# One rare-case block in place of two, and three reorderings, in a graph, attention and expert layer on one core

## The chip, the cores and the metric

The kernel runs on one core of a Trainium2 chip. The metric is the device time of one execution in microseconds (us). Before the change the median of three runs is 1005.16 us (1004.86 to 1005.45).

The engines of the core are named as in the profile: PE (TensorE, matrix products), with PEld for its weight loads; DVE (VectorE); ACT (ScalarE); POOL (GpSimd); SP (SyncE, which here only issues DMAs). A `q` after a name is that engine's instruction queue.

## The reference

The layer takes 625 nodes with 1024 features and 20000 edges (`src`, `dst`, sorted by `dst`).

```python
xn = layernorm(x)
x = x + gnn(xn, src, dst) + mix(xn)
x = x + ffn(layernorm(x))

# gnn: two layers, mean over the incoming edges
agg = segment_sum(h[src], dst); mean = agg / max(deg, 1)
h = relu(xn @ W_self0 + mean(xn) @ W_neigh0 + b0)
out = h @ W_self1 + mean(h) @ W_neigh1 + b1

# mix: linear attention, 16 heads of 64
q = softmax(x @ Wq, over a head's 64) / 8;  k = softmax(x @ Wk, over the nodes);  v = x @ Wv
out = (q @ (k.T @ v)) @ Wo + bo

# ffn: 8 experts, the best 2 of each node, and a shared expert
routed = sum over the node's 2 experts of p * (silu(xf @ w1[e]) @ w2[e])
shared = sigmoid(xf @ shared_gate_w) * ((silu(gate) * up) @ shared_down)
```

## The kernel before, in words

**Numbers in two parts.** Every operand of the large products is split into a high part, which ACT casts, and a low part, which DVE (in the experts' inputs POOL) makes by a subtraction. `split`, line 99, does both, so line 99 stands for a great many instructions that differ by their tile: `whi` and `wlo` are the two parts of a weight tile, `xnh` and `xnl` those of the normalised features, `xfh` and `xfl` those of the expert stage's input, `xs` those of an expert's rows, `he` those of an expert's hidden values. Each product is three matmuls: high by high, low weight by high, high weight by low.

**Weights.** All weights come from HBM in tiles of 512 KB through one list, `Stream`. SP issues the loads (line 121) into three buffers `wraw`; in the expert stage three more, `wmore`, are used in turn. `whi` and `wlo` have three buffers each. A load waits until a buffer's last reader, as a rule a `wlo` subtraction, is done.

**Order.** A scheduler fixes the order of instructions on every engine when the kernel is built, from priorities and the dependencies. Some instructions are held in the order of the program (`keep_in_program_order`, `keep` in the first stage), and `issue_after` puts one behind another. At run time each engine takes its queue in order. PSUM has eight banks which go round (`bank`), and the pool `tmp` has five buffers.

**Stages in order of time.**
1. Start (lines 433 to 462). The five node tiles are normalised (`first_stats`, `first_scale`, `first_norm`) and turned: `first_turn` calls `to_t` (line 283), which for each half g of the features does four PE transposes (line 288) into a bank and one `split` into `xnh`, `xnl`. Between them `keys_steps` runs pieces of the key product: `keys_step(s)` (lines 391 to 414) is twelve matmuls over four of the eight feature blocks, lines 405 to 407. The first steps need only node tiles 0 and 1 (256 columns) and run before the others are there. `keys_weights` takes a weight tile; the fourth goes into a tile named `fourth`. `turn_edges` (line 357, bank `psed`) turns the edge list. The last row of `x` is a DMA of its own (line 314).
2. One-hot counts of the edges (lines 485 to 539) among the rest of the key product and layer 0's self product. The counts are packed into `ath`, from which `dinv` and `degs` (inverse degrees) come. They are right unless two rare conditions hold, and `rare` is then not zero.
3. Queries, values, and the heads' 128 by 128 context blocks `cbd` (lines 742 to 749, bank `psc`).
4. **First If, line 752:** if `rare` is not zero, `recount` counts the edges anew with wider fields, and `inverse` makes the inverse degrees again. `values_load` (line 751) puts `rare` into a register of every engine. With the inputs here `rare` is zero and every engine jumps over the block.
5. `neighbours` (line 758): the product with `W_neigh0`, matmuls of `ts_half`, lines 209 to 211, bank `psg`.
6. Attention output (line 787), then the output projection (lines 801 to 813, bank `pso`). After its half 1, tile u=1, `low_step` is called: **second If, line 772**, which adds what the low parts of the counts contribute to layer 0, if `rare` is not zero. Besides, POOL loads rows of `x` into `xr` (line 809), adds the biases (line 810), and DVE adds the product (line 811).
7. Aggregation of layer 0 (line 828, bank `psag`), layer 1, with a third If at line 857.
8. The second layernorm; the shared expert's gate and up products (`ws_tile`, lines 226 to 228, banks `psga` and `psup`). Their columns come in two groups, node tiles 0 to 2 and tiles 3 and 4; tile 4 is turned last, right before the second group. Then `logits` (router and shared gate, `rwp` and `rwz`, bank `psr`, to `lgt`) for two column ranges `PARTS`, 0 to 313 and 314 to 625, then the routing.
9. The experts in the order `RANKS` = 0, 1, 2, 6, 3, 4, 5, 7 of their load, with room for 224 rows (ranks 0 to 2), 160 (3 to 5) or 128 (6, 7). `expert_wide` (lines 1193 on) takes ranks 0 to 5. Its first part forms the hidden values from w1 in four quarters (lines 1211 and 1215, bank `pse`); for each quarter `set` gathers the sum, then Silu, then `he` is split (lines 1220 to 1229). Its second part multiplies by w2 in two halves of four tiles, u = 0 to 3 (lines 1269 to 1271, bank `psy`; line 1246 for the rows beyond 128). A fourth If (line 1304) lies in the first expert.
10. The shared expert's down product and the final sums.

**The turns of the next expert's rows.** `Turn` (line 1016) holds the rows of the next expert. For a wide expert `Turn.step` does a DVE transpose of a block into `raw` (line 1046), and with the next step an ACT cast and a POOL subtraction into `xs`, line 99. A 224-row turn has two blocks of 512 columns and two of 384, a 160-row turn two of 512 and two of 128. The program calls `step` before each w2 tile of the running expert but the first. The scheduler is free as to where among DVE's other work the transposes go, as long as they keep their order.

## Time and profile before

| | us |
|---|---|
| median of three runs | 1005.16 |
| the profiled execution, its own time | 1006.07 |
| its span, first to last instruction | 1004.5 |
| PE busy | 994.2 |
| DVE busy | 601.4 |
| ACT busy | 394.4 |
| POOL busy | 144.5 |

The profiled execution took 0.91 us more than the median, and 1.57 us of it lie outside the span. The busy time of an engine is the time in which it has an instruction at work. A list of waits sums, for an engine and a line, the idle time before its instructions and names what ended it; `DVEq` or `PEq` with a line is the queue of that engine at a branch there. In a timeline row stand the start, the duration, the engine, the line, the operation with its tiles, a count if several equal ones follow each other, and in brackets the idle time before it. Matmuls overlap in the hardware, so the distance of two starts is what one costs, and it is shorter than the duration shown.

### The profile page before, as it was taken

To read this page: it belongs to the slowest core of one execution; us is meant where nothing else is said; L and a number is where in the kernel's file an instruction comes from. 1 tells how busy PE (TensorE), PEld (TensorE's weight loads), DVE (VectorE), ACT (ScalarE), POOL (GpSimd) and SP (SyncE) were. 2 spreads that over 40 slices of the span, in tenths; PEclk is the share of its full clock that TensorE was granted. 3 is DMA by queue.
4 is the path that set the end of the run, shared out by engine and by line. 5 is a ranking of instruction groups with operands and counts; after the bars stand their busy time and mean duration, and the time that the engine had idled before them with its cause. 6 is when DMAs were issued, how large, how long until landed. Compare 5 with 4: busy or idle time off the path is not lost. (4 is left out here: it accounts for less than half of the span.)

```text
span 1004.5 us, 14780 instructions
## 1 busy us (share of the span) xinstructions
PE 994.2 (99%) x5547; PEld 860.1 (86%) x5547; DVE 601.4 (60%) x1215; ACT 394.4 (39%) x577; POOL 144.5 (14%) x206
## 2 busy tenths in 40 slices
PE   9999999999999999999999999999999999999998
PEld 6999998888887779888878999997978787887886
DVE  7998745682333346423338355367678788877682
ACT  5533242231123212222116242265557576766610
POOL 1000011120100432200001002223032203110040
PEclk9999999999999999999999999999999999999999
DMA  8222227762321343322220125766977997887961
GB/s 238 60 65 64 85 100 257 251 235 86 95 84 64 105 157 124 124 83 84 66 82 2 46 81 173 241 205 207 266 244 217 292 357 237 280 297 253 339 249 64
DMA packets 111596, 164.69 MB, mean 164 GB/s; under 512 B 5948, under 2 KB 63686, under 8 KB 111512
## 3 DMA queue, kind: packets, MB, share of 16 engines
q1 hardware_dynamic: 97864, 118.38, 36.7%
q0 software_dynamic: 13456, 45.08, 13.6%
q8 instruction: 46, 0.75, 0.3%
q14 instruction: 38, 0.31, 0.1%
q10 hardware_dynamic: 192, 0.16, 0.0%
HBM read 133.19 MB, written 30.42 MB: 163 GB/s over the span
## 5 line engine op out<-in xcount | busy, mean ns | idle before, releaser
L99 DVE TENSOR_TENSOR wlo<-wraw,whi 128x1024 fp32r<-128x1024 f32 x148 | 186.0, 1257 | 247.0 <-ACT whi L99 237.8
L99 ACT CAST whi<-wraw 128x1024 fp32r<-128x1024 f32 x148 | 155.5, 1051 | 288.1 <-PE psg L211 76.2
L1215 PE MATMUL pse<-xs,whi 128*128 128x448 f32 (+1 forms) x384 | 109.2, 357 | 0.0
L99 DVE TENSOR_TENSOR wlo<-wmore,whi 128x1024 fp32r<-128x1024 f32 x67 | 82.1, 1226 | 25.8 <-ACT whi L99 23.3
L1211 PE MATMUL pse<-xs,wlo 128*128 128x224 f32 (+1 forms) x384 | 89.5, 254 | 0.6 <-DVE wlo L99 0.6
L99 ACT CAST whi<-wmore 128x1024 fp32r<-128x1024 f32 x67 | 70.4, 1051 | 42.5 <-PE psz L211 18.3
L405 PE MATMUL psk<-xnh,whi 128*128 128x384 f32 (+3 forms) x240 | 74.5, 312 | 0.3 <-ACT xnh L99 0.3
L406 PE MATMUL psk<-xnl,whi 128*128 128x384 f32 (+3 forms) x240 | 73.5, 306 | 0.6 <-DVE xnl L99 0.6
L407 PE MATMUL psk<-xnh,wlo 128*128 128x384 f32 (+3 forms) x240 | 73.5, 306 | 0.0
L1211 PEld LDWEIGHTS pse<-xs,wlo 128*128 128x128 f32 x384 | 72.0, 190 | 1.6 <-DVE wlo L99 0.8
L1215 PEld LDWEIGHTS pse<-xs,whi 128*128 128x128 f32 x384 | 69.1, 189 | 2.4
L1269 PE MATMUL psy<-whi,he 128*128 128x512 f32 (+1 forms) x176 | 69.5, 395 | 0.7 <-PEq L1304 0.7
L1270 PE MATMUL psy<-wlo,he 128*128 128x512 f32 (+1 forms) x176 | 69.4, 394 | 0.7 <-DVE wlo L99 0.7
L1271 PE MATMUL psy<-whi,he 128*128 128x512 f32 (+1 forms) x176 | 69.0, 392 | 0.0
L488 DVE TENSOR_SCALAR hot<-iota,srow,unit 125x128 f16<-125x128 f16 x160 | 49.6, 310 | 0.0
L406 PEld LDWEIGHTS psk<-xnl,whi 128*128 128x128 f32 x240 | 45.5, 190 | 0.8 <-DVE xnl L99 0.8
L405 PEld LDWEIGHTS psk<-xnh,whi 128*128 128x128 f32 x240 | 45.4, 190 | 0.6 <-ACT xnh L99 0.6
L407 PEld LDWEIGHTS psk<-xnh,wlo 128*128 128x128 f32 x240 | 45.4, 189 | 0.0
L99 POOL TENSOR_TENSOR xs<-raw,xs 128x512 fp32r<-128x512 f32 (+2 forms) x24 | 28.3, 1182 | 110.0 <-ACT xs L99 109.6
L487 DVE TENSOR_SCALAR hot<-iota,edt 125x128 f16<-125x128 f16 x160 | 39.8, 250 | 4.1 <-PE pa L505 4.1
L1269 PEld LDWEIGHTS psy<-whi,he 128*128 128x128 f32 (+1 forms) x176 | 31.9, 181 | 10.8 <-issue 1.1
L1270 PEld LDWEIGHTS psy<-wlo,he 128*128 128x128 f32 (+1 forms) x176 | 31.8, 181 | 10.0 <-DVE wlo L99 1.7
(361 smaller groups left out, 2367.2 us busy)
## 6 DMA issues: line engine op xcount, KB each, us to landing
wraw<-in_L_ffn_w_dram SPq DMA_DIRECT2D x65, 512.0 KB, 5.1
wmore<-in_L_ffn_w_dram SPq DMA_DIRECT2D x63, 512.0 KB, 5.2
xsd<-zt POOLq DMA_DIRECT2D x9, 1024.0 KB
wraw<-in_L_gnn_W_self_dram SPq DMA_DIRECT2D x16, 512.0 KB, 3.6
wraw<-in_L_gnn_W_neigh_dram SPq DMA_DIRECT2D x16, 512.0 KB, 3.8
wraw<-_ffn_shared_gate_up_dram SPq DMA_DIRECT2D x16, 512.0 KB, 3.9
wraw<-in_L_mix_Wk_dram SPq DMA_DIRECT2D x8, 512.0 KB, 6.7
wraw<-in_L_mix_Wq_dram SPq DMA_DIRECT2D x8, 512.0 KB, 3.6
```

Source lines behind the costliest of these rows:

```text
L99: return (order(nc.scalar.copy(hi, srcap)), order((eng or nc.vector).tensor_sub(lo, srcap, hi.bitcast(F32))))
L405: nc.tensor.matmul(ps[:, :n], wh[:, kt, :], xnh[:, kt, c], start=kt == 0, stop=False)
L406: nc.tensor.matmul(ps[:, :n], wh[:, kt, :], xnl[:, kt, c], start=False, stop=False)
L407: nc.tensor.matmul(ps[:, :n], wl[:, kt, :], xnh[:, kt, c], start=False, stop=kt == KT - 1)
L487: nc.vector.tensor_scalar(h[:ET, :WIN], iota[:ET, :WIN], edst[e], None, op0=ALU.is_equal)
L488: return nc.vector.tensor_scalar(h[:ET, WIN:], iota[:ET, :WIN], srow[e], unit[e].bitcast(F32), op0=ALU.is_equal, op1=ALU.mult)
L1211: nc.tensor.matmul(ps[a][:, :n], wl[:, k, c], xs[:, kt, 0, :], start=False, stop=False)
L1215: nc.tensor.matmul(ps[a][:, :2 * n], wh[:, k, c], xs[:, kt], start=kt == 0, stop=kt == KT - 1)
L1269: nc.tensor.matmul(acc, h(kt, 0), wh[:, k, :], start=kt == 0, stop=False)
L1270: nc.tensor.matmul(acc, h(kt, 0), wl[:, k, :], start=False, stop=False)
L1271: nc.tensor.matmul(acc, h(kt, 1), wh[:, k, :], start=False, stop=kt == KT - 1)
```

## The change

It has four parts.

1. The If at line 752 is taken out, and its content goes into the If in the output projection, which is now `rare_step`. The load of `rare` into the registers stands after `neighbours`. The block's code becomes shorter: the loop over the eight feature blocks is a loop at run time (`For_i`) with a copy `go` of the operand, and `recount` takes the degrees from a `reduce_sum` of the counts instead of matmuls over reloaded low parts. With these inputs the block is not entered, so what is in it is jumped over before and after.
2. `logits` takes the ranges as an argument. The first range is called right after tile 4 is turned, ahead of the second column group of gate and up; the second range stands where both stood.
3. In the start the first two tiles are turned half by half (tile 0 and 1 of g=0, then of g=1) instead of tile by tile; the first two key steps do the four matmuls of high by high, then the four with the low weights, then the four with the low features, instead of the three in turn for each block; and the second weight tile is taken before the statistics of node tile 2.
4. A DVE transpose of `Turn.step` is put behind the low part of the last weight tile taken (`st.low`) and behind the low part of the running expert's last `he` (`behind`).

In the instruction orders that the build gives, PE, DVE, ACT, POOL and SP differ around these places. Three of the moves are not in the diff's text. On SP the fifth load of `Wk` stands ahead of the one-row load of `x`, where it stood behind it. On PE four more matmuls on `fourth` stand ahead of tile 3's transposes. On ACT the square root for tiles 3 and 4 stands behind the first cast of tile 2's turn. In the experts the transposes, which stood among the additions into `set` and the `he` low parts, stand in one row behind them and behind `wlo` of w2's tile u=2, directly ahead of `wlo` of u=3; ACT's casts and POOL's subtractions of `xs` follow them.

```diff
-            split(r, hi, lo, eng, **order)
+            self.low = split(r, hi, lo, eng, **order)[1].ins
...
-    def to_t(nat, t, hi, lo, order=None, both={}):
-        for g in range(2):
+    def to_t(nat, t, hi, lo, order=None, both={}, parts=(0, 1)):
+        for g in parts:
...
-        for kt in range(4 * h, 4 * h + 4):
-            nc.tensor.matmul(ps[:, :n], wh[:, kt, :], xnh[:, kt, c], start=kt == 0, stop=False)
-            nc.tensor.matmul(ps[:, :n], wh[:, kt, :], xnl[:, kt, c], start=False, stop=False)
-            nc.tensor.matmul(ps[:, :n], wl[:, kt, :], xnh[:, kt, c], start=False, stop=kt == KT - 1)
+        kts = range(4 * h, 4 * h + 4)
+        terms = ((wh, xnh), (wh, xnl), (wl, xnh))
+        if s < 2:
+
+            order = [(kt, *terms[j]) for j in (0, 2, 1) for kt in kts]
+        else:
+            order = [(kt, *term) for kt in kts for term in terms]
+        for j, (kt, w, xt) in enumerate(order):
+            nc.tensor.matmul(ps[:, :n], w[:, kt, :], xt[:, kt, c], start=h == 0 and j == 0,
+                             stop=h == 1 and j == len(order) - 1)
...
-        first_turn(0)
-        first_turn(1)
+        for g in range(2):
+            for t in range(2):
+                first_turn(t, (g,))
+        keys_weights(1)
         first_stats(2)
-        keys_weights(1)
...
+            nc.vector.reduce_sum(degs[:, 0, ds(r, 1)], acc, axis=AX.X)
...
-        for t in range(NT):
-            pt = bank("psdt")
-            for s in range(NT):
-                al = tmp.tile([128, T], F32R, name="al", tag="tmp")
-                nc.gpsimd.dma_start(al[rows(s), rows(t)], atd[cols(s), cols(t)])
-                nc.tensor.matmul(pt[rows(t), :2], ath[rows(s), s, cols(t)], ones[rows(s), :2], start=s == 0, stop=False)
-                nc.tensor.matmul(pt[rows(t), :2], al[rows(s), rows(t)], ones[rows(s), :2], start=False, stop=s == NT - 1)
-            nc.vector.tensor_copy(degs[rows(t), 0, t:t + 1], pt[rows(t), 0:1])
...
-    rare_v = nc.values_load(rare[0:1, 0:1], min_val=0, max_val=2)
-    with tc.If(rare_v > 0, preferred_fallthrough_block=False):
-        recount()
-        inverse(0, NT - 1)
-        inverse(NT - 1, 1)
...
     neighbours(xnh, xnl, g0h, g0l)
-    def low_step(half, u, accs):
+    rare_v = nc.values_load(rare[0:1, 0:1], min_val=0, max_val=2)
+
+    def rare_step(half, u, accs):
...
         with tc.If(rare_v > 0, preferred_fallthrough_block=False):
+            recount()
+            inverse(0, NT - 1)
+            inverse(NT - 1, 1)
             for s in range(NT):
                 al = low_part(s)
-                for o in range(KT):
+                with tc.For_i(0, KT, 1) as o:
+                    go = tmp.tile([128, 128], F32R, name="go", tag="tmp")
+                    nc.scalar.copy(go[rows(s), :], g0h[rows(s), s, ds(o * 128, 128)].bitcast(F32))
...
-    def logits():
-        for c0, n in PARTS:
+    def logits(parts):
+        for c0, n in parts:
...
     to_t(by_k(xfn[rows(4), 4, :]), 4, xfh, xfl)
+
+    logits(PARTS[:1])
     ga.append(bank("psga"))
     up.append(bank("psup"))
     ws_tile(xfh, xfl, ga[1:], SPARTS[1:], w=wg)
     ws_tile(xfh, xfl, up[1:], SPARTS[1:], w=wu)
-    logits()
+    logits(PARTS[1:])
...
+            self.behind = st.low
...
-                tc.keep_in_program_order(nc.vector.transpose(
-                    raw.rearrange("p k (t r) -> p t k r", r=32), rows[:, :, k]))
+
+                with tc.issue_after(st.low), tc.issue_after(self.behind):
+                    tc.keep_in_program_order(nc.vector.transpose(
+                        raw.rearrange("p k (t r) -> p t k r", r=32), rows[:, :, k]))
...
-                    nc.vector.tensor_sub(h2[:, :, b0:b0 + m], s[:, :, a0:a0 + m], h2[:, :, a0:a0 + m].bitcast(F32))
+                    low_he = nc.vector.tensor_sub(h2[:, :, b0:b0 + m], s[:, :, a0:a0 + m], h2[:, :, a0:a0 + m].bitcast(F32))
             else:
-                split(s, h2[:, :, :n], h2[:, :, n:])
+                low_he = split(s, h2[:, :, :n], h2[:, :, n:])[1]
         nxt = nxt()
+        nxt.behind = low_he.ins
```

More of the change, by code (lines that the diff above doesn't have):

```diff
@@ L342, in first_norm, with first_turn @@
             keep(nc.scalar.activation(xts[p, t, :], xts[p, t, :], AF.Identity, bias=z, scale=y))
-    def first_turn(t):
-        return to_t(xts[rows(t), t, :].rearrange("p (k c) -> p k c", c=128), t, xnh, xnl, keep, dict(order=keep))
+    def first_turn(t, parts=(0, 1)):
+        return to_t(xts[rows(t), t, :].rearrange("p (k c) -> p k c", c=128), t, xnh, xnl, keep, dict(order=keep), parts)
     edges = edgep.tile([EP, 2, 2 * ET], F32, name="edges")
@@ L778, in low_step @@
                         c = slice(c0, min(c0 + n, N))
-                        nc.tensor.matmul(ps[:, :n], g0h[rows(s), s, o * 128:(o + 1) * 128], al[rows(s), c0:c0 + n],
-                                         start=True, stop=True)
+                        nc.tensor.matmul(ps[:, :n], go[rows(s), :], al[rows(s), c0:c0 + n], start=True, stop=True)
                         lt = tmp.tile([128, NP], F32, name="lt", tag="tmp")
                         nc.vector.tensor_mul(lt[:, c], ps[:, :min(n, N - c0)], dinv[:, c])
-                        nc.vector.tensor_add(hself[:, o, c], hself[:, o, c], lt[:, c])
+                        nc.vector.tensor_add(hself[:, ds(o, 1), c], hself[:, ds(o, 1), c], lt[:, None, c])
             hold(accs)
@@ L803, in gps_layer @@
         accs = [bank("pso") for _ in range(NT)]
-        ts_half(aoh, aol, accs, step=lambda u: low_step(half, u, accs))
+        ts_half(aoh, aol, accs, step=lambda u: rare_step(half, u, accs))
         for t in range(NT):
```

## The prediction

> **What bounds the kernel now.** The page's first two parts come first. They say whether one engine fills the span and at what clock.

> ```profile
> span 1004.5 us, 14780 instructions
> PE 994.2 (99%) x5547; PEld 860.1 (86%) x5547; DVE 601.4 (60%) x1215; ACT 394.4 (39%) x577; POOL 144.5 (14%) x206
> PEclk9999999999999999999999999999999999999999
> ```

> TensorE (PE) is busy for 99% of the span, and its granted clock stands in the highest digit throughout. No other engine passes 60%. So a change that leaves the executed matmuls as they are can win only what lies between matmuls. That the change leaves them can be read in the code: the block that it shortens isn't entered with these inputs (the trace has no instruction of `recount`), and the other three parts reorder. The next view is therefore the list of PE's waits: line, what it waited for, total us, times, longest.

> ```profile
> PE pswarm L252 <- DVE cold L249: 1.5, 1, 1.5
> PE psg L209 <- DVEq L752: 0.8, 1, 0.8
> PE psy L1270 <- DVE wlo L99: 0.7, 2, 0.4
> PE psy L1269 <- PEq L1304: 0.7, 1, 0.7
> ...
> PE psk L406 <- DVE xnl L99: 0.6, 1, 0.6
> ...
> PE pso L209 <- PEq L772: 0.5, 1, 0.5
> PE psk L405 <- ACT xnh L99: 0.3, 1, 0.3
> PE psga L226 <- ACT xfh L99: 0.2, 1, 0.2
> PE psga L227 <- DVE xfl L99: 0.2, 1, 0.2
> ```

> With 0.6 at line 1211 and 0.5 at line 857, not shown, that is the whole stock: 6.6 us. The change aims at the 0.8 (line 752), the two of the start (0.6 and 0.3), the two 0.2 of line 226/227 and the 0.7 of line 1270, 2.8 us as listed. A matmul's listed wait is shorter than what it costs in starts, as the timeline shows (start, duration, operation, idle before it), so I count by starts.

> ```profile
> 266.00 1.17 PE L746 MATMUL psc<-vnat,knat 128*128 128x128 f32 x9
> 267.99 0.47 PE L209 MATMUL psg<-whi,xnh 128*128 128x512 f32 x1 [0.82 <-DVEq L752]
> ...
> 372.43 0.50 PE L209 MATMUL pso<-whi,aoh 128*128 128x512 f32 x1 [0.54 <-PEq L772]
> ```

> **Part 1, one If in place of two.** Nine `psc` matmuls start 0.11 us apart from 266.00, so the next start was due at 267.00 and came at 267.99: 0.99 us lost at line 752. That goes. The If at line 772 remains: matmul 371.51 is followed by 372.43 where 0.23 is the rule, 0.70 lost, and the merged If stands there. The matmul that follows reads weights split long before, so nothing else is late there. Bounds: −0.70, what the shorter If costs, and −1.00; I take −0.99. The register loads of `rare` now come just before the merged block on every engine; ScalarE (ACT) and VectorE (DVE) have nothing due for over 5 us after their branches (next work at 371.9 and 373.0, branches before 367.6), and PE reached its compare at 367.7, 4 us before it mattered. GpSimd (POOL) stood 46.5 us at line 752 ahead of the first `xr` loads; that goes, and nobody waited for them. Its waits at line 772 (7.4 for DVE, 2.1 for PE) stay ahead of the second half's `xr`. Price of this queueing: 0, bounds 0 and +2.1, if PE's turn came to wait so.

> [...] The trace's two jumps, 0.99 and 0.70, both show a stall.

> **Part 2, half of the logits earlier.** After tile 4's transposes PE waits twice, 555.82 and 556.48.

> ```profile
> 555.82 0.38 PE L226 MATMUL psga<-xfh,whi 128*128 128x242 f32 x1 [0.19 <-ACT xfh L99]
> ...
> 556.48 0.38 PE L227 MATMUL psga<-xfl,whi 128*128 128x242 f32 x1 [0.17 <-DVE xfl L99]
> ```

> The excess over the rule of 0.11 is 0.35 and 0.33, together 0.68. The first half of the logits (columns 0 to 313, tiles 0 to 2, turned long before) is 16 matmuls of 0.145 us, 2.3 us of work that reads nothing of tile 4, and the stall needs about 1. `rwp` and `rwz` are ready at 550.7. So −0.68; bounds 0 (if a bank isn't free) and −0.68. The cover is the banks' earlier readers, which ended at 552.1 and 555.4; the second half's copy to `lgt` is no later.

> **Part 3, the start.**

> ```profile
> 13.52 0.38 PE L405 MATMUL psk<-xnh,whi 128*128 128x256 f32 x1 [0.34 <-ACT xnh L99]
> 14.47 0.38 PE L406 MATMUL psk<-xnl,whi 128*128 128x256 f32 x1 [0.56 <-DVE xnl L99]
> ...
> 17.31 0.45 PE L357 MATMUL psed<-ident,edges 80*125 80x80 f32 x3
> ...
> 24.49 0.81 DVE L340 TENSOR_SCALAR xts<-xts,lnt 128x1024 f32<-128x1024 f32 x1
> 25.88 1.52 PE L288 MATMUL pst<-ident,xts 128*128 128x128 f32 x13
> ```

> With half g=0 of both tiles first, ACT's first two casts of 0.51 from 11.91 end at 12.94, and the first matmul starts near 13.04 (before 13.52). The four `xnh` and four `wlo` products cover DVE's subtracts, which end at 15.02; 24 matmuls of 0.12 end at 15.92 where `psed` now starts at 17.31: PE is 1.39 ahead. But DVE is without a gap from 12.5 to 29.5. With the same instructions in another order `first_norm(3)` (line 340) still ends near 25.30, and tile 3's transposes behind it start at 25.3 to 25.6 against 25.88: about −0.38. The order after the change has four more `fourth` matmuls ahead of them (16, before 12), of which three fit, −0.36: −0.74 if DVE loses nothing. Two rows say that it may. ACT's square root for tiles 3 and 4 (22.46 before) now stands behind a cast of tile 2's turn, which PE reaches near 22.2: some +0.2. And SyncE's queue has the fifth `wk` load ahead of the last row of `x` (one row, issued at 12.81, landed at 17.9). That load waits for a `wraw` buffer, free when `wlo` of the second tile ends, now near 16.2, so the row is issued at 16.7; the 512 KB ahead of it took 3.4 to 4.9 us to land when issued at 17.57, so the row lands at 20 to 21.1. Its reader, the statistics of tile 4, stands at 20.95: late by 0 to 0.2. I take −0.5; bounds 0 and −1.39.

> **Part 4, turns behind low parts.** In a wide expert's w2 part, DVE does the next expert's transposes (line 1046), the set adds, `he` low parts and `wlo`; POOL subtracts `xs` low parts. PE stalls where `wlo` of the fourth tile (u3) is late: two places, 840.37 (0.53 by starts) and 875.80 (0.50), both with a 160-row host.

> ```profile
> 837.25 0.44 DVE L1046 STREAM_TRANSPOSE raw<-xb 128x128 f32<-128x128 f32 x1
> 837.62 1.55 DVE L1227 TENSOR_TENSOR he<-set,he 128x256 fp32r<-128x256 f32 x2
> ...
> 840.37 0.50 PE L1270 MATMUL psy<-wlo,he 128*128 128x512 f32 x1 [0.36 <-DVE wlo L99]
> ```

> Before, the transposes stand at 833.06, 834.32 and 837.25. Now they stand behind `wlo` of u2 and the last `he`, in one row ahead of `wlo` of u3. Worked forward from `whi` of u2 at 833.3 with these durations: `wlo` u2 to 835.6, `he` to 836.2, transposes 1.14 + 1.17 + 0.38 to 838.9. POOL's first `xs` subtract (1.31) then runs from 838.1 to 839.4. The trace shows what a POOL subtract does to a DVE operation beside it: the `he` pair took 1.55 with POOL's 2.14 at 836.95 beside it, and `wlo` at 735.66 took 1.53, where 1.2 is usual, with POOL's 1.36 running from 734.76. So `wlo` of u3 begins when POOL ends, and ends at 840.5, against need at 839.84: stall 0.7 in place of 0.53, +0.2 at each place. Without the clash it ends at 840.15, −0.15 each. Bounds for the two: −1.03 (all goes) and +1.8 (POOL's second subtract goes first too). I take +0.4. At the three 224-row hosts (`wlo` of u3 ended 692.01, 735.24 and 777.64, needed at 692.58, 735.81 and 778.98) the same row of transposes ends near 734.1 just as POOL's first subtract does: 0 if DVE gets in, stall 0.7 each at two places (third: slack 1.3) if POOL's second subtract does. I take 0; bounds −0.3 and +1.8.

> [...]

> **Sum.** −0.99 − 0.68 − 0.5 + 0.4 = −1.8. Unchanged are the waits of lines 857 and 1304, both ends of narrow experts and the warm-up. The profiled execution took 1006.07 (span 1004.5), 0.9 over the median of 1005.16; I subtract from the median: 1003.4.

> **The rivals.**
> 1. Everything aimed at goes: −0.99 − 0.68 − 1.39 − 1.03 = −4.1, 1001.1. For it: the parts each name a real wait. Against: DVE without a gap to 29.5, and transposes bunched ahead of the very `wlo` that was late.
> [...]
> 3. The start's gain is given back in full to DVE's chain, by the late row of `x` and the square root: −1.8 + 0.5 = −1.3, 1003.9.
> 4. Ends on the other side: the merged If holds up the output projection. POOL stands longer before the second half's `xr`, DVE's five additions of line 811 behind them keep PSUM banks from `psag`, and PE waits. Slower than before from 1.8 us lost there, at 6 us 1009. For it: DVE already waits 1.10 at 384.18 for a sum of POOL's. Against: PE shows no wait in this stretch after 372.43, and POOL is there first by the 46.5 us won.

> **How the numbers follow.** Chances: forecast 0.45 (own range 1002.4 to 1004.4), rival 1 0.17, rival 2 0.18, rival 3 0.12, rival 4 0.08. A measurement tells from no change what is over 0.2%, here 2.0 us: below 1003.15 is faster, above 1007.17 slower. Faster: nearly half of the forecast's and all of rival 1's, 0.38. Slower: most of rival 4, a little of rival 2, 0.08. Same: the rest, 0.54. The range leaves out one in ten at each side: 1001.4 (inside rival 1) to 1005.5 (lower part of rival 2).

> **What would show it.** Part 1: no wait for line 752, one of 0.5 to 0.8 at the merged If, the start after the last `psc` at 0.11. Part 2: no wait at `psga` of lines 226 and 227. Part 3: first `psk` at 13.0, `psed` at 15.9, tile 3's transposes at 25.3 to 25.6, and no wait of the tile 4 statistics for `x`. Part 4: line 1270's wait for `wlo` still there at the 160-row hosts; `wlo` of 1.5 us or more, or starting where a POOL subtract ends. I am wrong if the merged If costs over 2 us, or waits for `wlo` appear at the 224-row hosts.

## The result and the profile after

The change makes the kernel slightly slower. Median 1007.16 us (1005.82 to 1009.11, 14 runs) against 1005.39 (1004.72 to 1006.01, 14 runs) for the kernel before: ratio 1.0018, 95% interval 1.0011 to 1.0024. The forecast was 1003.4, with a range up to 1005.5.

The profiled execution of the changed kernel took 1007.03 us, against 1006.07 before. The page says that PE does the same work, and its list of waits says where the rest went. (The diff shifts line numbers: before's 405 to 407 are now one line, 412; 772 is 768, 1046 is 1051, 1269 to 1271 are 1275 to 1277, 1304 is 1310.)

```profile
span 1005.5 us, 14766 instructions
PE 995.1 (99%) x5547; PEld 861.1 (86%) x5547; DVE 605.8 (60%) x1215; ACT 394.6 (39%) x577; POOL 150.2 (15%) x206
PEclk9999999999999999999999999999999999999999
```

```profile
PE pso L209 <- issue: 3.6, 1, 3.6
PE pswarm L252 <- DVE cold L249: 1.5, 1, 1.5
PE psy L1275 <- PEq L1310: 0.7, 1, 0.7
PE psx L209 <- PEq L857: 0.4, 1, 0.4
PE psy L1276 <- DVE wlo L99: 0.3, 2, 0.2
```

Eleven rows have become five. All the waits that the change aimed at are gone or smaller, and so are two that it did not aim at (line 1211, and a little of line 857). One row is new, 3.6 us at the first `pso` matmul behind the merged If, and it takes back nearly all that was won: the list sums to 6.5 us, before to 6.6. By the list alone nothing would be lost. What ended the new wait is "issue": no semaphore, no engine. PE itself did not issue. The timeline at this place (start, duration, operation, idle before it):

```profile
369.76 0.39 PE L211 MATMUL pso<-whi,aol 128*113 128x512 f32 x1
373.71 0.50 PE L209 MATMUL pso<-whi,aoh 128*128 128x512 f32 x1 [3.56 <-issue]
374.04 0.40 PE L210 MATMUL pso<-wlo,aoh 128*128 128x512 f32 x1
...
375.20 0.61 PE L209 MATMUL pso<-whi,aoh 128*128 128x512 f32 x1
375.60 0.63 PE L210 MATMUL pso<-wlo,aoh 128*128 128x512 f32 x1
376.03 0.63 PE L211 MATMUL pso<-whi,aol 128*128 128x512 f32 x1
...
378.59 0.41 PE L211 MATMUL pso<-whi,aol 128*128 128x512 f32 x1
378.84 0.39 PE L209 MATMUL pso<-whi,aoh 128*128 128x512 f32 x1
```

Two losses are to be seen, and no list of waits can show the second. The start that was due 0.23 after 369.76 comes 3.72 late. And from 375.20 to 378.59 the starts lie 0.42 apart where 0.23 is the rule, eight of them, 1.6 us more. The cause of the second is in the table by stages, whose columns are the window, its length, PE's busy time with its matmuls, the granted clock (1.00 is full speed), DMA share and GB/s. First the changed kernel, then the one before:

```profile
369.00:374.00 5.00, 1.45 (x7) 1.00 0.34 102
374.00:379.00 5.00, 5.00 (x16) 0.66 0.76 263
379.00:384.00 5.00, 5.00 (x24) 1.00 0.02 6
```

```profile
369.00:374.00 5.00, 4.46 (x20) 1.00 0.84 281
374.00:379.00 5.00, 5.00 (x24) 1.00 0.41 126
379.00:384.00 5.00, 5.00 (x24) 1.00 0.29 93
```

The granted clock falls to 0.66 in the stage behind the pause: 16 matmuls in 5 us instead of 24. The page's row of 40 slices does not show it (a slice is 25 us), and PE counts as busy in it. That PE's pause is its own branch is told by the instructions of the If's line (number, shortest, median and longest duration in ns, first and last start). The second branch of each pair is the jump over the block:

```profile
L768 PEldq COMPARE_BRANCH  x2: 98/1702/3306, 366.5 to 370.3; - x2
L768 DVEq COMPARE_BRANCH  x2: 51/53/55, 364.9 to 365.8; - x2
```

```profile
L772 PEldq COMPARE_BRANCH  x2: 64/175/286, 367.7 to 372.1; - x2
```

The jump took 3306 ns, and 286 over the block of before; that over the first block of before took 304. (With two branches the median is their mean, so the smallest and the largest are the two.)

The small gain at line 857 is a jump too: it took 296 ns before and 185 now.

The account from profile to profile, by how far the starts of each stage are shifted against before:

| stage | won (−) or lost, us | forecast |
|---|---|---|
| start, to the end of the key product | −0.68 | −0.5 |
| first If gone | −1.07 | −0.99 |
| merged If: pause 3.72 in place of 0.70 | +3.02 | 0 |
| merged If: low clock behind it | +1.6 | none |
| If at line 857 | −0.12 | 0 |
| logits | −0.93 | −0.68 |
| experts | −0.91 | +0.4 |
| sum | +0.9 | −1.8 |

### The profile page after: what moved, and what is told of

The parts are those of the page before. It is cut to its first block, busy times and chain, and to the rows that moved or that the text cites. A ratio compares the mean times of both kernels' runs of the same rounds, so it can differ in the third digit from the quotient of the medians.

```text
span 1005.5 us, 14766 instructions
## 1 busy us (share of the span) xinstructions
PE 995.1 (99%) x5547; PEld 861.1 (86%) x5547; DVE 605.8 (60%) x1215; ACT 394.6 (39%) x577; POOL 150.2 (15%) x206
## 5 line engine op out<-in xcount | busy, mean ns | idle before, releaser
L99 DVE TENSOR_TENSOR wlo<-wraw,whi 128x1024 fp32r<-128x1024 f32 x148 | 188.7, 1275 | 251.3 <-ACT whi L99 244.6
L99 ACT CAST whi<-wraw 128x1024 fp32r<-128x1024 f32 x148 | 155.5, 1051 | 288.5 <-PE psg L211 75.1
L99 DVE TENSOR_TENSOR wlo<-wmore,whi 128x1024 fp32r<-128x1024 f32 x67 | 87.0, 1298 | 24.4 <-ACT whi L99 22.6
L99 ACT CAST whi<-wmore 128x1024 fp32r<-128x1024 f32 x67 | 70.4, 1050 | 43.6 <-PE psz L211 18.5
L99 POOL TENSOR_TENSOR xs<-raw,xs 128x512 fp32r<-128x512 f32 (+2 forms) x24 | 35.7, 1506 | 117.4 <-ACT xs L99 117.3
```

Source lines behind the costliest of these rows:

```text
L99: return (order(nc.scalar.copy(hi, srcap)), order((eng or nc.vector).tensor_sub(lo, srcap, hi.bitcast(F32))))
```

## The experiments

The first question is whether the jump is slow because of what is in the block, because of what else waits at the If, or because of where its target lies. PE's instructions can be counted in the built programs (a matmul counts as a weight load and a matmul, of which the page has 5547 each). Counted so, the block that PE jumps over has 248 instructions at the first If of before, 176 at the second, and 314 in the merged one. It is shorter than both together, and longer than either. One of the profile's two instruction queues, q8, fetches 16 KB at a time (0.75 MB in 46 fetches):

```profile
q8 instruction: 46, 0.75, 0.3%
```

Between two of them the trace of before has 256 of PE's instructions in the median, 230 to 268 in the middle half of the 45 cases, and that of the changed kernel 254. So q8 is taken as PE's queue, and a page of code, as what one fetch brings is called here, is taken to hold 256 instructions; both are estimates of the author from these counts. The theory of the page, which the runs below test: a jump of 314 passes over a whole page when it starts late in its own, and then its target is not there. From the fetches around the If, the changed kernel's branch stands some 205 to 255 instructions into its page (this place is worked out from the fetch times, not read from a row); it passes over a whole page from 198 on.

**Part 1 undone.**

```diff
+    rare_v = nc.values_load(rare[0:1, 0:1], min_val=0, max_val=2)
+    with tc.If(rare_v > 0, preferred_fallthrough_block=False):
+        recount()
+        inverse(0, NT - 1)
+        inverse(NT - 1, 1)
...
-        ts_half(aoh, aol, accs, step=lambda u: rare_step(half, u, accs))
+        ts_half(aoh, aol, accs, step=lambda u: low_step(half, u, accs))
```

> Parts 2, 3 and 4 stay, part 1 is undone: two Ifs as before. All theories put the loss at the merged If and expect it gone, with the wait at the first If back at 0.8: about 0.7 won at the start, 0.9 at the logits, 0.9 in the experts, so 2.5 us under before, near 1002.9. If instead one of parts 2 to 4 brought the loss with it, it stays above before.

Measured: 1003.51 us (10 runs), ratio 0.9979 (0.9970 to 0.9989). Both Ifs cost what they did before, and the profile is 2.8 ahead at the end: 1.25 at the start (in this execution the warm-up itself ends 0.5 earlier), 0.93 at the logits, 0.73 in the experts. Parts 2 to 4 are a gain, and the whole loss is in part 1.

**Part 1 alone, on the kernel before.**

```diff
-    rare_v = nc.values_load(rare[0:1, 0:1], min_val=0, max_val=2)
-    with tc.If(rare_v > 0, preferred_fallthrough_block=False):
-        recount()
-        inverse(0, NT - 1)
-        inverse(NT - 1, 1)
...
-        ts_half(aoh, aol, accs, step=lambda u: low_step(half, u, accs))
+        ts_half(aoh, aol, accs, step=lambda u: rare_step(half, u, accs))
```

> Part 1 alone, on the kernel before. Theory of the page: the jump's target on PE is two pages of 256 instructions on, so the branch takes 3.3 us in place of 0.3 and the clock is lowered behind it: 4.6 lost at the merged If, 1.1 won at the first, 3.5 over before, near 1008.9. Theory of a late partner (POOL or DVE reach the If late): the same sum, but with a semaphore named as what ended the wait, and not the branch itself.

Measured: 1009.06 us (7 runs), ratio 1.0029 (1.0017 to 1.0040). The wait is 4.0 and again ends by "issue"; the jump takes 3786 ns:

```profile
L760 PEldq COMPARE_BRANCH  x2: 98/1942/3786, 367.4 to 371.2; - x2
```

So no partner is late, the branch itself takes the time, and the other three parts have no hand in it.

**The same work, 68 instructions further on.** The block, its content and what is executed stay; only PE's code ahead of it grows.

```diff
     for i in range(WARM):
-        nc.tensor.matmul(psw, cold[:, :128], cold, start=i == 0, stop=i == WARM - 1)
+        for a, b in ((0, 256), (256, 512)) if i < 34 else ((0, 512),):
+            nc.tensor.matmul(psw[:, a:b], cold[:, :128], cold[:, a:b], start=True, stop=True)
```

> The changed kernel, with each of the 34 warm-up matmuls done in two of half the width: 68 more instructions on PE ahead of the If, the same work. Theory of the page: the branch then stands some 40 instructions into its page instead of some 220, its target is in the next page, the branch takes 0.3, no low clock behind it: 3.6 under before, near 1001.6. Theory that the merged block is slow to jump because it is long or has loops in it: nothing changes, near 1007.2 with a branch of 3.3.

Measured: 1006.19 us (1004.68 to 1007.62, 10 runs), ratio 1.0006 (0.9996 to 1.0015), where 1001.6 was expected. The theory holds for the branch; the time that was expected from it did not come. The jump, and then the kernel's two longest waits:

```profile
L769 PEldq COMPARE_BRANCH  x2: 98/246/393, 365.8 to 369.6; - x2
```

```profile
PE psag L829 <- DVE xr L812: 2.7, 1, 2.7
PE pswarm L253 <- DVE cold L249: 1.5, 1, 1.5
```

The jump takes 393 ns, and the pause at the merged If is 0.8. A merged block is thus not slow by itself. But a new wait stands 14 us later: `psag`, a bank of the aggregation, waits for DVE's additions of `xr`. In DVE's queue a small memset of `hth` stands ahead of the last three of them, and waits 4.8 us for POOL:

```profile
DVE hth L298 <- POOL xr L811: 4.8, 1, 4.8
```

```profile
370.08 0.58 POOL L810 DMA_DIRECT2D xr<-in_x_dram  x1 [12.12 <-PEq L769]
...
385.06 1.25 POOL L811 TENSOR_TENSOR xr<-xr,bsums 113x512 f32<-113x512 f32 x1 [3.10 <-DMA xr<-in_x_dram]
```

POOL's first load of the second half's `xr` waits 12.1 us, until PE is past the If. Before, three of the six loads were issued from 367.8 on, ahead of PE's jump at 372.1. In this execution, the fastest of the ten, the granted clock is 1.000; in six of the ten it is 0.998 or less, with times up to 1007.62. That the wait at `psag` brings the low clock in these is shown by no trace. The guess rests on the kernel below that is without this wait: its six runs have 0.999 or 1.000.

**Eight instructions instead of 68** (the same edit with 4 in place of 34).

> The changed kernel with 4 warm-up matmuls in two of half the width, 8 instructions more on PE. Theory of the page: the branch stays in the last quarter of its page, the target two pages on, the branch takes 3.3 as before the shift, near 1007. If splitting warm-up matmuls helped by itself, or any shift did, the branch would be short.

Measured: 1006.83 us (1 run). The branch is long as before, and neither split warm-up matmuls nor a shift as such cure it:

```profile
L769 PEldq COMPARE_BRANCH  x2: 98/1882/3666, 366.0 to 369.8; - x2
```

**A longer block in the kernel before.** No merging, no loops; 200 instructions that are never executed.

```diff
+        pad_ps = bank("pspad")
+        for i in range(100):
+            nc.tensor.matmul(pad_ps[:, :128], ones, ones, start=i == 0, stop=i == 99)
         inverse_degrees()
```

> The kernel before, with 100 more matmuls (200 instructions) in the block of the first If, which is not entered. Theory of the page: its target moves from the next page to the one after, and the first If costs 3 us more by its branch, and up to 1.7 by a lower clock behind it: 3 to 5 over before, near 1009. Theory that merging or its loops are the cause: as before, 1005.2.

Measured: 1010.43 us (4 runs), ratio 1.0050 (1.0033 to 1.0067). The branch grows from 304 ns to 3426, and the pause and the low clock behind it are the picture of the changed kernel, at another If. Branch, matmuls (start to start 0.43 from 272.11 on) and stages:

```profile
L755 PEldq COMPARE_BRANCH  x2: 98/1762/3426, 265.2 to 266.9; - x2
```

```profile
270.51 0.47 PE L209 MATMUL psg<-whi,xnh 128*128 128x512 f32 x1 [3.78 <-issue]
...
272.53 0.63 PE L210 MATMUL psg<-wlo,xnh 128*128 128x512 f32 x1
272.96 0.63 PE L211 MATMUL psg<-whi,xnl 128*128 128x512 f32 x1
```

```profile
265.00:270.00 5.00, 1.72 (x16) 1.00 0.12 46
270.00:276.00 6.00, 5.49 (x17) 0.72 0.58 183
276.00:280.00 4.00, 4.00 (x20) 1.00 0.00 0
```

With the shift of 68 this settles the cause: the place of the jump and its target decides, once by 68 instructions ahead of it with the block untouched (3306 to 393 ns), once by 200 more in the block with the rest untouched (304 to 3426 ns). That places count in pages of 256 stays the author's estimate.

That a fetch lies in each long jump can also be read from the traces. In the changed kernel one instruction fetch falls between 369.5 and 374:

```profile
q8 instruction: 1, 0.02, 1.3%
```

It starts at 371.31, 0.96 us after the jump began, and takes 0.93. So it is in all five kernels with a long jump: one fetch starts 0.88 to 0.96 into the jump, and the jump ends 1.40 to 1.52 us after it has landed. The fetches took 0.93, 0.93, 1.03, 1.32 and 1.44 us, and the jumps, in the same order, 3266, 3306, 3426, 3666 and 3786 ns: the slower the fetch was, the longer the jump. Behind the short jumps at these Ifs a fetch starts too, but 1.0 to 1.9 us after the jump began, when PE is past it.

**The second wait: `xr` in buffers of its own.** `xr` came from the pool `tmp`, five buffers that go round, and the merged block's tiles (`hrare`, `aj`, `go`) come from it as well and are read by PE inside the If. A load into such a buffer has to wait until PE is past the If, 12.1 us above. (Of the second block of before PE reads only `al` from this pool, and one load waited 2.1 us for PE there.) Here the second half's five tiles lie in the unused rest of the tile that holds the biases; the shift of 68 stays.

```diff
-    bsums = big.tile([128, 2, D], F32, name="bsums", tag="big")
+    xrs = big.tile([128, 9, 512], F32, name="bsums", tag="big")
+    bsums = xrs[:, :4, :].rearrange("p (a b) c -> p a (b c)", b=2)
...
-            xr = tmp.tile([128, 512], F32, name="xr", tag="tmp")
+            xr = xrs[:, 4 + t, :] if half else tmp.tile([128, 512], F32, name="xr", tag="tmp")
```

> The kernel with the 68 instructions more, and the second half's xr tiles in the unused rest of the tile that holds the biases, no longer in buffers that the merged block's instructions also use. Theory that POOL's loads of xr wait for PE to pass the If because they share buffers with the block: the loads start some 3 us earlier, the wait of psag for DVE's additions (2.7) goes, and the kernel ends near 1002.0. Rival, that the loads are late by POOL's own queue or by the DMA traffic: the 2.7 stays, near 1006.

Measured: 1002.32 us (1001.70 to 1002.76, 6 runs), ratio 0.9968 (0.9956 to 0.9981), faster than both kernels, and by ratio below the one with part 1 undone (0.9979), with intervals that overlap. POOL's sums for the second half are done at 358, ahead of the If, and the wait at `psag` is gone:

```profile
347.11 6.01 POOL L812 TENSOR_TENSOR bsums<-bsums 128x512 f32<-128x512 f32 x4
357.06 1.28 POOL L812 TENSOR_TENSOR bsums<-bsums 113x512 f32<-113x512 f32 x1 [2.93 <-DMA bsums<-in_x_dram]
```

```profile
PE pswarm L253 <- DVE cold L249: 1.5, 1, 1.5
PE psy L1277 <- PEq L1312: 0.7, 1, 0.7
PE psy L1278 <- DVE wlo L99: 0.7, 2, 0.5
PE pso L209 <- PEq L769: 0.6, 1, 0.6
PE psx L209 <- PEq L859: 0.4, 1, 0.4
```

**The edit of `xr` without the shift.**

> The changed kernel with the same edit to xr alone. The long branch on PE stays, since its place is not moved: a branch of 3.3, low clock behind it, near 1007, no gain from xr. If the loads of xr were what held PE up at the If, the time would fall by 3 or more.

Measured: 1007.78 us (10 runs), ratio 1.0019 (1.0010 to 1.0029). The branch takes 3266 ns and nothing is won. The two costs of part 1 lie over each other: while PE stands in its branch, POOL and DVE catch up. Taking away either alone leaves the other (1006.19 and 1007.78, against 1007.16); only both together give 1002.32.

**Part 4 alone**, on the kernel before: the lines with `behind` and `issue_after` of the diff.

> Part 4 alone, on the kernel before. By the changed kernel's profile: the waits at line 1270 shrink from 0.5 to 0.3 at the two 160-row hosts, none appears at the 224-row hosts, 0.4 us won in all. By the prediction: they grow by 0.2 each.

Measured: 1006.06 us (1 run), and its profile ends 0.01 from that of before. The waits for `wlo` at the two 160-row hosts cost 0.33 and 0.66 by starts, 0.53 and 0.50 before; none appears at the 224-row hosts. The second varies from kernel to kernel with part 4 in it: 0.34 in the changed kernel, 0.33 with part 1 undone, 0.67 and 0.91 in the two with `xr` apart. At these two places part 4 is worth about nothing, between −0.4 and +0.2 in the profiles. The rest of the 0.9 won in the experts, but for 0.15 of small losses, is the wait of line 1211 (0.70 by starts in the profile before, at 816.47): it is absent from the two kernels that have part 1 alone or the longer block alone, so part 4 is not its cause. In the profile before, its load was under way for 6.97 us from 807.06; why it is late there and not elsewhere stayed open. No part aimed at it, so that the changed kernel is without it is luck.

## Why the prediction was wrong

**Part 1: the step that failed** is "the merged If stands there" with the 0.70 of the shorter block, and "Price of this queueing: 0, bounds 0 and +2.1". I took the price of a jump from the two jumps of the trace as if it belonged to an If, and didn't count what is jumped over. "What the shorter If costs" took the merged block for a shorter one. Its code is shorter than 248 + 176 together; at 314 it is longer than either, and longer than the 256 taken for one fetch. The gain at the first If was right (1.07 for 0.99). The loss at the merged one was 3.02 by the branch and 1.6 by the clock behind it, 4.6 together, where 0 stood and 2.1 was the bound.

**Both jumps of the trace were the cheap case.** That they "both show a stall" was taken for the price of any jump. Their branches took 304 and 286 ns; the five long ones here took 3266 to 3786 ns, each with an instruction fetch in it.

**The clock was not in the sum at all.** A low clock followed the pauses of 3.7 to 4.2 us, in five kernels, each time seven or eight starts 0.43 apart instead of 0.23 (in the changed kernel the granted clock is 0.50 from 375.20 to 378.61); behind the pauses of 0.7 to 1.0 in the kernel before there is none, and the windows there show 1.00. Of the 14 runs of the changed kernel the fastest, 1005.82, is the only one with a granted clock of 1.000.

**Rival 4 had the place and the side, and the wrong mechanism.** It said that the merged If holds up the output projection through POOL, `xr`, line 811 and `psag`. That chain is real: 2.7 us when the branch is cheap. In the changed kernel it is covered by the branch. Its argument against, that POOL is "there first by the 46.5 us won", failed because the loads share buffers with the block, which makes them wait for PE and not for POOL's own turn.

**Part 2** was right, a little small: no `psga` wait is left, −0.93 for −0.68. **Part 3** was right in its mechanism: the first `psk` starts at 13.08, `psed` at 16.06 instead of 17.31, and most of this is given back at tile 3's transposes, which start at 25.63 (said: 25.3 to 25.6). Four more `fourth` matmuls are done by then, where three were counted, and the end stands at −0.68 for −0.5. The late square root showed as said: DVE's reciprocal behind it starts at 23.77 instead of 23.51. The row of `x` was issued at 16.65 and wasn't late; its reader starts at 21.02, with no wait for it. One reading was wrong and did no harm: in the profile before DVE does have a gap, 0.63 us ahead of 27.14, but none up to the end of `first_norm(3)` at 25.30, on which the working rests.

```profile
13.08 0.74 PE L412 MATMUL psk<-xnh,whi 128*128 128x256 f32 x4
...
16.06 0.56 PE L357 MATMUL psed<-ident,edges 80*125 80x80 f32 x4
...
25.63 1.58 PE L288 MATMUL pst<-ident,xts 128*128 128x128 f32 x13
```

**Part 4** was wrong by sign and small: +0.4 was said, −0.36 came at these two places. The clash was as described. The last two rows are DVE's and POOL's:

```profile
837.08 2.58 DVE L1051 STREAM_TRANSPOSE raw<-xb 128x512 f32<-128x512 f32 x3
839.54 1.82 DVE L99 TENSOR_TENSOR wlo<-wmore,whi 128x1024 fp32r<-128x1024 f32 x1
...
838.98 4.93 POOL L99 TENSOR_TENSOR xs<-raw,xs 128x512 fp32r<-128x512 f32 x3 [19.97 <-ACT xs L99]
```

`wlo` of u=3 took 1.82, about what is left when it starts as POOL's first subtraction ends (that one took 1.29, so 838.98 + 1.29 = 840.27, + 1.1 = 841.4, and it ended at 841.36). But the row of transposes starts 0.4 us earlier than I had worked out: at 837.08, where the 836.2 of my working would be 837.45, since DVE's rows ahead stand 1.25 later than before. So `wlo` was ready 0.4 earlier against PE's need, and the stall was 0.3 in place of 0.7. At two of the 224-row hosts DVE got in first, as taken; at the third `wlo` took 1.87 (from 778.05) beside POOL's first subtraction, and PE did not wait, since there was slack. No run shows the loss at all five hosts for which the range and the chance of rival 2 left room: the changed kernel's list has two waits for `wlo`, 0.3 us in all.

## What to carry to other kernels

Before moving or merging blocks that are jumped over, count the instructions that the bounding engine skips and compare them with what one instruction fetch brings, 256 by the estimate here: the skips of 248 and 176 took 0.3 us in the kernel before, one of 314 took 0.3 to 3.8 by its place, and 3.0 to 3.6 us more of pause on PE cost another 1.4 to 1.7 by the clock behind it. Ask also which buffers the skipped block shares with work around it: loads into them waited here for PE to pass the If, 12.1 us, though nothing in the block ran. And when the largest wait goes and the time does not, look for the wait that it had covered.
